# A three-layer graph network on one core: node-times-weight products as three float32r products instead of float32, with the last group's products moved in between them

## The chip, the core and the metric

The kernel runs on one core of a Trainium2 chip. The metric is the device time of one launch in microseconds (us); lower is better. The engines named below are TensorE (PE, with its weight loads shown apart as PEld), VectorE (DVE), ScalarE (ACT), GpSimd (POOL) and SyncE (SP), which here only issues DMAs. Each engine works through its own list of instructions in order.

## What is computed

2500 nodes with 256 features each, 80000 edges `src -> dst`, three layers with weights of 512 x 256, and a last weight of 1024 x 256:

```python
h = max(layernorm(x), 0)
xs = [h]
for W, b in ((W0, b0), (W1, b1), (W2, b2)):
    m = concatenate([h[dst], h[src] - h[dst]]) @ W + b     # per edge
    h = relu(segment_sum(m, dst) / max(count(dst), 1))     # per node
    xs.append(h)
out = x + concatenate(xs) @ Wf + bf
```

The kernel counts the edges into a matrix A (nodes by nodes, count of edges) and works on whole nodes: a layer is A times (nodes times the lower half of W), scaled, plus nodes times the difference of both halves; the last weight is applied layer by layer.

## The kernel before

The nodes are padded to 20 tiles of 128 (`NT`), and kept transposed in `hT` (feature rows, node columns) in float32. The columns of A are cut into five groups of at most 504 (`GS`); four of them form two pairs, and the fifth, with 486 columns, is `alone`. A float32 product appears in the trace as two matmul instructions; a float32r one, whose operands keep fewer bits, as one.

The time falls into stages, each bound to the next by the values of `hT`:

- Up to about 62 us: edges, layer norm, the first node products, and the first counts.
- To 204.97 us: layer 0. Counts are made with bf16 one-hot products, and multiplied with the node products at once. The node products are kept as two float32r parts, `zh` and `zl`, whose sum is the float32 value.
- Layers 1 and 2, each in three parts, in the loop that starts at line 1194:
  - **nodes**: `nodes_pair` (line 1000) for ten pairs of tiles `t, t + Q`. PE multiplies `hT` with the lower half of W (`ws[l][1]`, tile name `wb`) into one PSUM bank, ACT scales it with `share` into `zf`, ACT and DVE split it into `zh` and `zl`, DVE forms four sums of its quarters (`combine`, line 989), which are split into `sh` and `sl`. `final` (line 758) multiplies the same tiles of `hT` with that layer's part of the last weight (`wfs[l]`, tile name `wf`) and DVE adds the product to `acc`, the output being gathered.
  - **lone group**: `Alone` (line 1115), first in the `Stream` (line 1158): 80 float32r matmuls of the split nodes with the fifth group, then the group's own product with `ws[l][0]` (tile name `wt`) and its relu on ACT.
  - **pairs**: `Pair` (line 1028), 2 x 5 x 7 steps: a seven-product scheme of the kind of Strassen and Winograd. A step has four float32r matmuls of 504 columns. Its moving operand, a `block`, is made by ACT (a cast of what SP loaded into `staged`) or by DVE (a sum of two such blocks), up to six steps ahead; `ready` has seven buffers for it. At the last of each five, `take` (line 1089) adds the products up into `hT`.
- `final(L, t)` for all 20 tiles, with the output's DMAs.

`tick` (line 1207) adds the bias `bf_sb` to `acc` on DVE in four instructions, in layer 1 at steps 6 to 9, which are steps of the lone group. All calls through `DVEo`, `ACTo`, `POOLo`, `PEo` and `SPo` keep the order of the program on their engine, and the names `tmp`, `staged`, `block` and `bank` are pools of buffers: an instruction that writes one waits until its last reader is done.

Of the kernel before, what the change touches and what calls it, by code (L numbers as in the profile page):

```python
# [313 lines left out]
def by_windows(ctx: ExitStack, tc: tile.TileContext, x, src, dst, Ws, bs, Wf, bf, out, missing):  # L314
# [122 lines left out]
    wfs = [None] * (L + 1)  # L437

    def load_wb(l, queue=SP):
        ws[l] = wpool.tile([P, DC, D], F32, name="wt"), wpool.tile([P, DC, D], F32, name="wb", bufs=1)  # L440
        queue.dma_start(ws[l][1], Ws[l][D:2 * D, :].rearrange("(c p) d -> p c d", p=P))
# [4 lines left out]
    def load_wf(l, queue=SP):  # L446
        wfs[l] = wpool.tile([P, DC, D], F32, name="wf", bufs=1)
        queue.dma_start(wfs[l], Wf[l * D:(l + 1) * D, :].rearrange("(c p) d -> p c d", p=P))
# [309 lines left out]
    def final(l, *ts):  # L758
        po = bank()
        for i, t in enumerate(ts):  # L760
            for c in range(DC):
                PEo.matmul(po[:, i * D:(i + 1) * D], hT[:, c, t * P:(t + 1) * P], wfs[l][:, c, :],
                           start=(c == 0), stop=(c == DC - 1))
        for i, t in enumerate(ts):
            DVEo.scalar_tensor_tensor(acc[:, t, :], po[:, i * D:(i + 1) * D], share[:, t:t + 1], acc[:, t, :],
                                      op0=OP.mult, op1=OP.add)
            if l == L:
                n = P if t < NT - 1 else LAST
                SPo.dma_start(out[t * P:t * P + n, :], acc[:n, t, :])

# [148 lines left out]
    ps_left = ctx.enter_context(tc.tile_pool(name="ps_left", bufs=4, space=PSUM))  # L919
    head[0].close()  # L920
    ps_right = ctx.enter_context(tc.tile_pool(name="ps_right", bufs=4, space=PSUM))
# [46 lines left out]
    def bank():  # L968
        ps.append(ps_left if ps[-1] is ps_right else ps_right)
        return ps[-1].tile([P, 512], F32, name="bank")  # L970

    tmps = ctx.enter_context(tc.tile_pool(name="tmps", bufs=6))
    stage = ctx.enter_context(tc.tile_pool(name="stage", bufs=3))
# [7 lines left out]
    S3, S5, S2, S4 = range(4)  # L981
    SEVEN = (("x", 0, 0), "b11"), (("x", 0, 1), "b21"), (("s", S4), "b22"), (("s", S5), "r1"), \
        (("s", S2), "r2"), (("s", S3), "r3"), (("x", 1, 1), "r4")
# [5 lines left out]
    def combine(to, x):  # L989
        DVEo.tensor_sub(to[:, S3:S5 + 1, :], x[:, 0::3, :], x[:, 1:2, :].to_broadcast([P, 2, P]))  # L990
        DVEo.scalar_tensor_tensor(to[:, S2, :], to[:, S5, :], -1.0, x[:, 0, :], op0=OP.mult, op1=OP.subtract)
        DVEo.scalar_tensor_tensor(to[:, S4, :], x[:, 2, :], -1.0, to[:, S2, :], op0=OP.mult, op1=OP.subtract)

    def both_of(z, t):
        return z[:, t % 2, :Q * D].rearrange("p (i q d) -> p i q d", i=2, d=D)[:, :, t // 2, :]

    def sums_of(z, t):
        return z[:, t % 2, t // 2 * 2 * D:(t // 2 + 1) * 2 * D]

    def nodes_pair(l, t):  # L1000
        two = t, t + Q
        pz = bank()
        for i, u in enumerate(two):
            for c in range(DC):
                PEo.matmul(pz[:, i * D:(i + 1) * D], hT[:, c, u * P:(u + 1) * P], ws[l][1][:, c, :],
                           start=(c == 0), stop=(c == DC - 1))
        zf = tmp()
        for i, u in enumerate(two):
            part = slice(i * D, (i + 1) * D)
            if u == NT - 1:  # L1010
                DVEo.scalar_tensor_tensor(zf[:, part], pz[:, part], share[:, u:u + 1], brow[:, l % 2, :],
                                          op0=OP.mult, op1=OP.add)
            else:
                ACTo.activation(zf[:, part], pz[:, part], AF.Copy, scale=share[:, u:u + 1])
        ACTo.copy(both_of(zh, t), zf.rearrange("p (h d) -> p h d", h=2))
        raw = tmp()
        combine(raw.rearrange("p (s n) -> p s n", s=4), zf.rearrange("p (s n) -> p s n", s=4))
        ACTo.copy(sums_of(sh, t), raw)
        DVEo.tensor_sub(both_of(zl, t), zf.rearrange("p (h d) -> p h d", h=2), both_of(zh, t).bitcast(F32))
        final(l, *two)  # L1020
        DVEo.tensor_sub(sums_of(sl, t), raw, sums_of(sh, t).bitcast(F32))

    def part_of(what, z, j):
        if what[0] == "x":
            return tile_of((zh, zl)[z], j + what[2] * Q)[:, what[1] * P:(what[1] + 1) * P]
        return sums_of((sh, sl)[z], j)[:, what[1] * P:(what[1] + 1) * P]

    class Pair:
# [6 lines left out]
        def load(self, c):  # L1035
            st = stage.tile([P, 4, 2, GS], BF16, name="staged")
            j = 2 * c
            for i, g in enumerate(pairs[self.i]):
                SPo.dma_start(st[:, 2 * i:2 * i + 2, :, :],
                              a_dram[g].rearrange("p (h j) n -> p h j n", h=2)[:, :, j:j + 2, :])  # L1040
            return st

        def make(self, c, what, st, made):
            to = made[what] = ready.tile([P, 2, GS], F32R, name="block")
            b11, b21, b12, b22 = (st[:, i, :, :] for i in range(4))
# [4 lines left out]
            elif what == "r2":  # L1050
                DVEo.tensor_add(to, made["r1"].bitcast(F32), b22)
            elif what == "r3":
                DVEo.tensor_sub(to, made["r2"].bitcast(F32), b11)
            else:
                DVEo.tensor_add(to, made["r2"].bitcast(F32), b21)

        def own_sum(self, i):
# [7 lines left out]
            elif i == 2:  # L1065
                r["r3"] = tmp()[:, :GS]
                DVEo.tensor_sub(r["r3"], r["r2"], hT[:, 0, one])
# [21 lines left out]
        def take(self, what):  # L1089
# [6 lines left out]
            elif what == "b22":  # L1096
                self.f = tmp()[:, :GS]
                DVEo.tensor_add(self.f, m, self.e1)
# [16 lines left out]
    class Alone:  # L1115

        def __init__(self, l):
            self.l = l
            self.c0, self.n = group_of(alone)

        def load(self, c):
            st = stage.tile([P, 4, 2, GS], BF16, name="staged").rearrange("p a b n -> p (a b) n")[:, :4, :]
            SPo.dma_start(st, a_dram[alone][:, 4 * c:4 * c + 4, :])
            return st

        def make(self, c, i, st, made):
            made[i] = ready.tile([P, 2, GS], F32R, name="block")
            ACTo.copy(made[i], st[:, 2 * i:2 * i + 2, :])

        def multiply(self, c, i, made):  # L1130
            n = self.n
            if c == 0 and i == 0:
                self.banks = [bank(), bank()]
            for k in range(2):
                t = 4 * c + 2 * i + k
                for o in range(DC):
                    for z in (zh, zl):
                        unit[0] = PEo.matmul(self.banks[o][:, :n], tile_of(z, t)[:, o * P:(o + 1) * P],
                                             made[i][:, k, :n], start=(t == 0 and z is zh), stop=False)
            if c == 4 and i == 1:  # L1140
                for o in range(DC):
                    for cc in range(DC):
                        PEo.matmul(self.banks[o][:, :n], ws[self.l][0][:, cc, o * P:(o + 1) * P],
                                   hT[:, cc, self.c0:self.c0 + n], start=False, stop=(cc == DC - 1))
                for o in range(DC):
                    ACTo.activation(hT[:, o, self.c0:self.c0 + n], self.banks[o][:, :n], AF.Relu)

    def steps_of(l):
        steps, loads = [], []
        for p in Alone(l), Pair(l, 0), Pair(l, 1):  # L1150
            for c in range(5) if isinstance(p, Pair) else (0, 1, 3, 2, 4):
                loads.append((p, c))
                made = {}
                for part, what in SEVEN if isinstance(p, Pair) else ((None, 0), (None, 1)):
# [3 lines left out]
    class Stream:  # L1158
# [19 lines left out]
        def run(self, tick, between):  # L1178
            for n, (m, p, c, part, what, made) in enumerate(self.steps):
                for then in between.get(n, ()):  # L1180
                    then()
                self.make(n + LEAD + 1)
                if isinstance(p, Pair):
                    if c == 2:
                        p.own_sum([w for _, w in SEVEN].index(what) - 2)
                    p.multiply(c, part, what, made)
                    if c == Q // 2 - 1:
                        p.take(what)
                else:
                    p.multiply(c, what, made)  # L1190
                tick(n)

    DVEo.tensor_sub(ws[1][0], ws[1][0], ws[1][1])
    for l in range(1, L):
        stream = Stream(l)
        stream.load(3)
        for i, t in enumerate(range(Q) if l == 1 else [6, 0, 1, 2, 3, 4, 5, 7, 8, 9]):
            nodes_pair(l, t)
            if i == 6:
                stream.make(2)  # L1200
        load_wf(l + 1, SPo)
        if l + 1 < L:
            load_b(l + 1, SPo)
            load_wb(l + 1, SPo)
            load_wt(l + 1, SPo)

        def tick(n):
            if l == 1 and 6 <= n < 10:
                part = acc[:, (n - 6) * 5:(n - 5) * 5, :]
                DVEo.tensor_add(part, part, bf_sb.unsqueeze(1).to_broadcast([P, 5, D]))  # L1210

        def sums_of_w():
# [46 lines left out]
```

## Time and profile before

Three runs: 493.4, 493.45 and 494.22 us, the median 493.45. The profiled execution took 493.74 us; its span, from the first to the last instruction, is 491.9.

| Stage (from the trace) | from us | to us | PE busy | PEld busy | DVE busy | ACT busy | POOL busy |
|---|---|---|---|---|---|---|---|
| nodes, layer 1 | 204.97 | 239.30 | 34.33 | 30.22 | 27.27 | 21.44 | 0 |
| lone group, layer 1 | 239.30 | 259.90 | 20.60 | 16.57 | 13.60 | 11.82 | 0 |
| nodes, layer 2 | 336.40 | 370.70 | 34.30 | 30.19 | 28.57 | 22.80 | 0 |
| last products | 467.60 | 485.60 | 17.45 | 15.01 | 10.36 | 1.98 | 0 |

A row is a stretch of the span, and its entries are the time in it in which each engine had an instruction at work. PE is busy through every one of these stretches; the other engines have time to spare in each. PE's durations overlap[...], so a matmul's cost is read from the distance of two starts ("pitch"), not from its duration. Over the whole span the granted TensorE clock was 0.997 of full speed.

### The profile page before, as it was taken

The numbers are of one execution on the slowest core, as the hardware profiler recorded it, in microseconds if no ns is written. First come the engines' busy times: TensorE is split into PE (matmuls) and PEld (weight loads), VectorE is DVE, ScalarE is ACT, GpSimd is POOL, SyncE is SP. The second block draws the span as 40 slices with busy tenths as digits, with TensorE's granted clock in tenths as the row PEclk, the third lists the DMA queues.
The fourth block names the chain that finished last, engine by engine and source line by source line (L and its number), as shares of the span: only waits on it lengthen the run. The fifth ranks groups of instructions, "written<-read, shape, count | busy, mean of one in ns | idle before, by whom it ended". The sixth has DMA issues, their size and how long they took to land.

```text
span 491.9 us, 7411 instructions
## 1 busy us (share of the span) xinstructions
PE 481.7 (98%) x2776; PEld 384.0 (78%) x2776; DVE 366.6 (75%) x767; ACT 241.3 (49%) x445; POOL 43.2 (9%) x66
## 2 busy tenths in 40 slices
PE   8999999999999999999999999999999999999994
PEld 4888888778778778788887867868888788688683
DVE  8999988888888861087955959867883469689552
ACT  5676677653734340257745445425578344364010
POOL 3682006100101000000000000000000000000000
PEclk9999999999999999999999999999999999999998
DMA  9310098970914609300472552420015534340033
GB/s 289 106 43 1 2 203 153 204 150 0 184 29 86 127 5 205 130 1 7 141 253 85 168 168 76 136 85 1 1 42 162 202 121 142 111 144 26 0 116 100
DMA packets 26679, 51.73 MB, mean 105 GB/s; under 512 B 1945, under 2 KB 22378, under 8 KB 26602
## 3 DMA queue, kind: packets, MB, share of 16 engines
q1 hardware_dynamic: 19850, 33.54, 20.8%
q0 software_dynamic: 5856, 16.51, 17.6%
q10 hardware_dynamic: 928, 1.11, 0.7%
q8 instruction: 24, 0.39, 0.3%
q14 instruction: 21, 0.17, 0.1%
HBM read 35.69 MB, written 16.10 MB: 105 GB/s over the span
## 4 chain that ended last, share of the span: by engine, by line
PE 91%; DVE 3%; POOL 3%; DMA 1%; issue 1%; SPq 0%; POOLq 0%
PE bank L282 87%; PE pz L282 3%; POOL acc L282 2%; DMA acc<-in_x_dram 1%; DVE st L282 1%; POOL ed L282 1%; POOL es L282 0%; DVE mv L282 0%; PE turned L282 0%; DVE zl L282 0%; DVE rs L282 0%; DVE off L282 0%; DVE away L282 0%; DVE one_m L282 0%; DVE kn L282 0%
## 5 line engine op out<-in xcount | busy, mean ns | idle before, releaser
L282 ACT CAST block<-staged 128x1008 fp32r<-128x1008 bf16 x80 | 77.6, 1031 | 40.9 <-issue 38.2
L282 PE MATMUL bank<-a,zh 128*128 128x504 f32 (+1 forms) x200 | 84.3, 422 | 0.0
L282 PE MATMUL bank<-block,zh 128*128 128x504 f32 (+1 forms) x200 | 83.4, 417 | 0.0
L282 DVE TENSOR_TENSOR one_m<-iota_m,key_m 128x1024 bf16<-128x1024 bf16 (+1 forms) x105 | 72.0, 686 | 14.1 <-PE bank L282 14.0
L282 ACT CAST a<-bank 128x480 fp32r<-128x480 f32 (+1 forms) x105 | 52.9, 565 | 59.3 <-PE bank L282 59.3
L282 PE MATMUL bank<-a,zl 128*128 128x504 f32 (+1 forms) x200 | 77.8, 389 | 0.0
L282 PE MATMUL bank<-block,zl 128*128 128x504 f32 (+1 forms) x200 | 77.6, 388 | 0.0
L282 DVE TENSOR_TENSOR block<-block,staged 128x1008 fp32r<-128x1008 f32 x60 | 70.8, 1205 | 4.9 <-PE bank L282 1.7
L282 PE MATMUL bank<-block,sh 128*128 128x504 f32 x160 | 68.7, 429 | 0.0
L282 DVE TENSOR_TENSOR one_n<-iota_n,key_n 128x480 bf16<-128x480 bf16 (+1 forms) x210 | 66.9, 359 | 0.0
L282 PE MATMUL bank<-block,sl 128*128 128x504 f32 x160 | 62.5, 391 | 0.0
L282 PE MATMUL bank<-wf,hT 128*128 128x256 f32 x240 | 55.2, 379 | 0.0
L282 PEld LDWEIGHTS bank<-wf,hT 128*128 128x128 f32 x240 | 45.6, 190 | 6.2
L282 DVE TENSOR_TENSOR block<-staged 128x1008 fp32r<-128x1008 bf16 x20 | 24.1, 1205 | 32.1 <-PE bank L282 32.1
L282 PEld LDWEIGHTS <-one_m 128*128 128x128 bf16 x834 | 39.1, 98 | 9.6 <-issue 3.2
L282 PEld LDWEIGHTS bank<-a,zh 128*128 128x128 f32 x200 | 37.8, 189 | 10.7 <-issue 2.6
L282 PEld LDWEIGHTS bank<-block,zh 128*128 128x128 f32 x200 | 37.7, 188 | 10.2 <-issue 3.2
L282 PEld LDWEIGHTS bank<-block,zl 128*128 128x128 f32 x200 | 37.6, 188 | 10.2 <-issue 3.2
L282 PEld LDWEIGHTS bank<-a,zl 128*128 128x128 f32 x200 | 37.7, 189 | 9.0 <-issue 2.6
L282 PE MATMUL bank<-one_n,one_m 128*128 128x120 bf16 x834 | 44.2, 208 | 0.0
L282 PE MATMUL bank<-wb,hT 128*128 128x256 f32 x160 | 37.8, 379 | 0.0
L282 PEld LDWEIGHTS bank<-block,sl 128*128 128x128 f32 x160 | 30.1, 188 | 9.7 <-issue 3.7
(144 smaller groups left out, 574.6 us busy)
## 6 DMA issues: line engine op xcount, KB each, us to landing
staged<-a_dram SPq DMA_DIRECT2D x50, 504.0 KB
a_dram<-a POOLq DMA_DIRECT2D x20, 630.0 KB, 7.5
out_dram<-acc SPq DMA_DIRECT2D x19, 128.0 KB
acc<-in_x_dram POOLq DMA_DIRECT2D x3, 640.0 KB, 11.8
wf<-in_L_gnn_Wf_dram SPq DMA_DIRECT2D x4, 256.0 KB
acc<-in_x_dram SPq DMA_DIRECT2D x1, 896.0 KB
acc<-in_x_dram ACTq DMA_DIRECT2D x1, 768.0 KB
wb<-in_L_gnn_W_dram SPq DMA_DIRECT2D x3, 256.0 KB
```

The source lines that it names most:

```text
L282: return self.tc.keep_in_program_order(call(*args, **kwargs))
```

## The change

The diff has four parts.

1. **Products.** A row of `hT` is cut into a high part and a rest, both short enough for float32r (`Split`: three parts, high, low, and a combination of both), and so are the weights (`Forms`: three parts). Three float32r matmuls then give what a float32 matmul gave (`times`). The weight `wb` and the last weight's part `wf` lie side by side in one tile (`raws`), so one matmul has 512 columns: the left 256 become the nodes' product, the right 256 the output's. In layer 1 the first two pairs of tiles are still multiplied in float32 (`times_whole`). The last stage has `wf` alone, 256 columns.
2. **Order of nodes and lone group.** A pair is now the tiles `2q, 2q+1`. In step i of twelve, PE multiplies the i-th pair of tiles and then the lone group's blocks with the nodes of step i-2; the lone group is no longer part of the `Stream`.
3. **Engines.** `combine` in the nodes (now three instructions) and the subtraction in `Split.low` are on POOL; the bias is added on POOL in layer 1 at steps 2, 6, 10 and 14 of the pairs. Some splits and the forms of the next stage are made during the last steps of the pairs.
4. **Buffers.** The PSUM banks are handed out anew for nodes (six, and two for the lone group) and pairs (eight); `stage` has four buffers instead of three, and `Split` takes its parts from it; a pair's load takes four neighbouring tiles of a group instead of two and two.

The signs of the seven-product scheme change with the order of the quarters; its steps and sizes do not.

```diff
     def load_wb(l, queue=SP):
-        ws[l] = wpool.tile([P, DC, D], F32, name="wt"), wpool.tile([P, DC, D], F32, name="wb", bufs=1)
+        raws[l] = wpool.tile([P, DC, 2, D], F32, name="wbf", bufs=1)
+        ws[l] = wpool.tile([P, DC, D], F32, name="wt"), raws[l][:, :, 0, :]
...
-    def combine(to, x):
-        DVEo.tensor_sub(to[:, S3:S5 + 1, :], x[:, 0::3, :], x[:, 1:2, :].to_broadcast([P, 2, P]))
-        DVEo.scalar_tensor_tensor(to[:, S2, :], to[:, S5, :], -1.0, x[:, 0, :], op0=OP.mult, op1=OP.subtract)
-        DVEo.scalar_tensor_tensor(to[:, S4, :], x[:, 2, :], -1.0, to[:, S2, :], op0=OP.mult, op1=OP.subtract)
+    def combine(to, x, V):
+        V.tensor_sub(to[:, M3:S5 + 1, :], x[:, 1::2, :], x[:, 0:2, :])
+        V.tensor_sub(to[:, S2, :], to[:, M3, :], x[:, 3, :])
+        V.tensor_add(to[:, M4, :], to[:, S2, :], x[:, 2, :])
...
+    class Split:
...
+        def high(self):
+            ACTo.activation(self.parts[0], self.h, AF.Copy, scale=DOWN)
+        def low(self, V):
+            V.tensor_sub(self.parts[1], self.h, self.parts[0].bitcast(F32))
+        def across(self, V):
+            V.scalar_tensor_tensor(self.parts[2], self.parts[1].bitcast(F32), -E12, self.parts[0].bitcast(F32),
+                                   op0=OP.mult, op1=OP.add)
+    class Forms:
...
+        def high(self):
+            ACTo.activation(self.parts[0], self.raw, AF.Copy, scale=C1 * DOWN)
+        def low(self):
+            for c in range(DC):
+                self.V.scalar_tensor_tensor(self.rest[c], self.raw[:, c, :], C1, self.parts[0][:, c, :].bitcast(F32),
+                                            op0=OP.mult, op1=OP.subtract)
...
+    def times(to, split, i, forms):
+        for c in range(DC):
+            for k in range(3):
+                PEo.matmul(to, split.parts[k][:, c, i * P:(i + 1) * P], forms.parts[k][:, c, :],
+                           start=(c == 0 and k == 0), stop=(c == DC - 1 and k == 2))
...
+    def split(q, V=POOLo):
+        sp = splits[q] = Split(q)
+        sp.high()
+        sp.low(V)
+        sp.across(DVEo)
...
     for l in range(1, L):
+        order = orders[l]
+        whole = 2 if l == 1 else 0
+        lone = Alone(l, order, banks(6, 2))
+        if l == 1:
+            load_alone(0, order)
+            split(order[whole])
+            forms = Forms(flat(l), 512, DVEo, [tmp(), tmp()])
+            forms.high()
+            forms.low()
+            forms.scaled()
+            forms.across()
+            forms.last()
...
+        for i in range(Q + LAG):
+            if 0 < i <= Q:
+                lone.make(i - 1)
+            if i < Q:
+                q = order[i]
+                n = Nodes(l, q)
+                n.multiply(None if i < whole else splits.pop(q), forms, flat(l))
+                if i + AHEAD_H < Q and i % 2 == 1:
+                    load_alone((i + 1) // 2, order)
+                n.parts()
+                n.combine(POOLo)
+                if i + AHEAD_H < Q and order[i + AHEAD_H] not in splits:
+                    split(order[i + AHEAD_H])
+                pending.append(n)
+            if i and pending:
+                pending.pop(0).sums()
+            if i >= LAG:
+                lone.multiply(i - LAG)
+            if i == Q - 1:
+                load_alone(Q // 2 - 1, order)
+                stream.load(3)
+        stream.make(2)
+        lone.end()
...
         def tick(n):
-            if l == 1 and 6 <= n < 10:
-                part = acc[:, (n - 6) * 5:(n - 5) * 5, :]
-                DVEo.tensor_add(part, part, bf_sb.unsqueeze(1).to_broadcast([P, 5, D]))
+            if l == 1 and 2 <= n < 18 and n % 4 == 2:
+                part = acc[:, (n - 2) // 4 * 5:(n + 2) // 4 * 5, :]
+                POOLo.tensor_add(part, part, bf_sb.unsqueeze(1).to_broadcast([P, 5, D]))
...
+            if n in (49, 56):
+                split(after[(n - 49) // 7])
+            if n == 63:
+                if l + 1 < L:
+                    load_alone(0, after)
+                else:
+                    split(after[3])
+            if n == 65:
+                split(after[2])
...
-    for t in [*range(7), NT - 4, NT - 3, NT - 2, NT - 1, *range(7, NT - 4)]:
-        final(L, t)
+    order = orders[L]
+    for i, q in enumerate(order):
+        po, sp = bank(), splits.pop(q)
+        for k in range(2):
+            times(po[:, k * D:(k + 1) * D], sp, k, forms)
+        for k in range(2):
+            t = 2 * q + k
+            add_to_acc(t, po[:, k * D:(k + 1) * D])
+            n = P if t < NT - 1 else LAST
+            SPo.dma_start(out[t * P:t * P + n, :], acc[:n, t, :])
+        for k in order[i + 1:i + 4]:
+            if k not in splits:
+                split(k)
```

`Nodes.parts` has the ACT and DVE work of `nodes_pair` without the sums (two scalings and the cast to `zh` on ACT, the subtraction to `zl` and two additions to `acc` on DVE), `Nodes.sums` the cast to `sh` and the subtraction to `sl`. The methods of `Forms` come in the order `high` (ACT), `low` (DVE, two instructions of 512 columns), `scaled` (ACT, two), `across` (DVE, two), `last` (ACT, two). The forms of the next stage are made by them in `tick` at steps 64, 66 and 67.

## The prediction

> **What bounds the kernel now.** I read first the page's shares and slices, then the chain of waits, then the stretches and the order of time where the change works.
>
> ```profile
> PE 481.7 (98%) x2776; PEld 384.0 (78%) x2776; DVE 366.6 (75%) x767; ACT 241.3 (49%) x445; POOL 43.2 (9%) x66
> ...
> PE   8999999999999999999999999999999999999994
> ...
> PEclk9999999999999999999999999999999999999998
> ...
> PE 91%; DVE 3%; POOL 3%; DMA 1%; issue 1%; SPq 0%; POOLq 0%
> ```
>
> PE is busy in every slice, at full clock, and the chain of the end is PE for 91%: from 62 us to 485 it is one piece. So a matmul saved in these stages is time saved, until another engine is late. The order of time gives what a matmul costs:
>
> ```profile
> 336.38 1.89 PE L282 MATMUL bank<-wb,hT 128*128 128x256 f32 x8
> 338.10 1.89 PE L282 MATMUL bank<-wf,hT 128*128 128x256 f32 x8
> ```
>
> ```profile
> 371.13 0.39 PE L282 MATMUL bank<-block,zl 128*128 128x486 f32 x1
> 371.35 0.38 PE L282 MATMUL bank<-block,zh 128*128 128x486 f32 x1
> ...
> 467.62 17.43 PE L282 MATMUL bank<-wf,hT 128*128 128x256 f32 x80
> ```
>
> Eight float32 instructions of 256 columns start every 1.726 us: 0.216 each, two to a product. A float32r matmul (the zl and zh rows) of 486 columns has a pitch of 0.220; in the pairs, 504 columns, 0.229. Per column that is 0.454 ns against 2 x 0.216 / 256 = 1.69 for a float32 product: three float32r products are 1.36, a fifth less.
>
> **The PE sum.** A tile now takes 8 instructions for `wb` and `wf`: 1.726 us. New: two feature halves x 3 x 512 columns x 0.454 = 6 x 0.232 = 1.39. Saved 0.334 a tile; 16 tiles in layer 1 (four stay float32, at 512 columns as dear as before) and 20 in layer 2: **12.0 us**. In the last stage a tile falls from 4 x 0.216 = 0.863 to six matmuls of 256 columns. No row has that width in float32r. Below, 256 x 0.454 = 0.116; above, the duration of its weight load, 0.190, if it can't overlap. The transposes have loads of the same 128 columns at a pitch of 0.108, so the stream should decide; as the excess over 2.4 columns per ns was 18 ns at both 486 and 504 columns, I take 256 / 2.4 + 18 = 0.125. Saved 0.863 - 0.75 = 0.113, x 20 = **2.3 us**. The stall of 0.19 before each lone group (pitch 0.41 for 0.22) goes too: 0.4. PE sum: **-14.7 us**. The lone group's 80 matmuls and its own product are only moved.
>
> **What replaces it.** In a step of the new nodes PE needs 12 x 0.232 + 8 x 0.220 = 4.54 us. Against that, by pitch from the rows of the old nodes:
> - ACT: two scalings 0.87, casts to zh and sh 0.5 each, Split.high like a cast 0.5, one lone block 0.94: 3.3. Hidden.
> - DVE: zl and sl 0.6 each, two additions to acc 0.79, Split.across about 0.66 (the 512-column two-input rows): 2.65. Hidden, but in order: across waits for POOL's low, and sl and the next zl stand behind it.
> - POOL: 256 + 128 + 128 columns of combine, 512 of low. POOL has run no two-input instruction in this trace. The nearest row is its normalisation, one tensor in:
>
> ```profile
> L282 POOL TENSOR_SCALAR acc<-acc,rs,off x16: 550/707/1469, 15.3 to 39.4; 128x256 f32<-128x256 f32 x16
> ```
>
> ```profile
> 22.86 2.18 POOL L282 TENSOR_SCALAR acc<-acc,rs,off 128x256 f32<-128x256 f32 x2
> ```
>
> ```profile
> 22.11 0.68 DVE L282 TENSOR_TENSOR one_m<-iota_m,key_m 128x1024 bf16<-128x1024 bf16 x1
> 22.71 0.64 DVE L282 TENSOR_TENSOR one_n<-iota_n,key_n 128x480 bf16<-128x480 bf16 x2
> 23.26 0.97 DVE L282 TENSOR_TENSOR one_m<-iota_m,key_m 128x1024 bf16<-128x1024 bf16 x1
> ```
>
> Undisturbed it takes 0.55 for 256 columns (2.15 ns each), beside DVE's two-input compares up to 1.47, and the compare takes 0.97 instead of 0.68 as POOL runs: they get in each other's way. Two inputs cost between the row's 2.15 and twice that, 4.3 ns. The Trainium skill (GPSIMD Engine Reference, 3.1 Elementwise) says 2.6 cycles per element for a two-input instruction, an estimate of 2.17 ns; I take this, the low end, as it names the very instruction, with 0.1 each on top: 1024 x 2.17 + 0.4 = **2.6 us**, plus at most two waits of 0.53 for DVE: 3.7 of 4.54. Hidden. The same page's 4.1 (Engine selection) speaks against the change: elementwise work of two inputs belongs on VectorE, POOL being about twice as slow. By it moving combine costs more than it frees; the old nodes' rows say DVE would have 2.65 + 1.0 (combine) + 0.6 (low) = 4.25 of 4.54, hardly any room, so POOL is the better place as long as its 3.7 holds.
>
> Where PE waits all the same:
> - **Start of layer 1: +2.3.** The forms' buffers come free only as layer 0 ends. ACT does relu, Split.high, forms; DVE waits for POOL's first low (1.2), then low, across: about 7 us, just what the two float32 pairs take (4 x 1.726 = 6.9). But behind the forms on ACT's queue stand the evacuations of pairs 0 and 1 and the next Split.high, 3.9 us; then POOL, low of pair 3 behind combine of pair 1, 2.2; across 0.8: 13.9 us after layer 0. PE is there at 6.9 + 2.78 + 1.76 = 11.4. Layer 2 has three splits made before: +0.4. No bound below zero; above, with POOL at 4.3 ns, 6 and 3.5.
> - **Bias on POOL: +3.1.** Four instructions of 1280 columns, 2.9 us each. They wait for no step of the pairs, so they run when POOL is free after the last combine, some 5 us before the pairs begin, just when DVE makes the first four sums of blocks (1.2 each, two SBUF inputs). The row: a POOL instruction of 0.55 cost the compare 0.29, half its time. With two inputs read I take three quarters: 2.1 us each, 8.6 in all, if one gets in ahead of each sum. DVE has 10.6 us for 5.2 of work: 8.6 - 5.4 = 3.2 late. The Trainium skill (SBUF — State Buffer, Who interferes with whom) has an exclusive lock for the whole instruction: 4 x 2.9 - 5.4 = 6. If the half holds: 5.8 - 5.4, 0.4. I take 3.1, and the ends 0 and 6. The old place, DVE in the lone group, cost nothing, as DVE was idle there.
> - **End of the pairs: +0.7 each layer.** At steps 49 and 56 DVE waits for POOL's low (1.2 + across 0.66), twice; the blocks are five steps ahead, 4.5 us, DVE has 1.5 us to spare in seven steps of 6.4 and the own sums need 2.7. Forms (2.6 us on DVE) come when no block is left to make.
> - **Last stage: +0.6.** DVE has 0.79 for every pair and 0.66 for six splits, ACT and POOL one instruction, PE 1.5. Only the fifth split, behind two relus on ACT, is late.
>
> The loads on SP's queue change in order, not in bytes; the first load of the pairs is asked for some 8 us before its use, beside a stage buffer that a split frees. The output's DMAs follow 15 us of additions instead of 17; the tail of 6.3 us behind the last addition stays.
>
> **Sum**: -14.7 + 2.3 + 0.4 + 3.1 + 1.4 + 0.6 = -6.9. The profiled execution of before took 493.74 (span 491.9), so 486.8; it lay 0.3 above the median, so I say **486.6 us**.
>
> **Rivals.**
> 1. *Everything hidden*: POOL nearer 1.5 ns, the lock cheap, the bias free. -14.7 + 2.3 = -12.4: **481 us**. For it: the undisturbed POOL row, and DVE's slack in all stages.
> 2. *POOL becomes the bound* in nodes: 1024 x 3 ns + 0.4 + waits of 1.06 = 4.54, so it decides from 3 ns on, and there the gain is about gone. At 4 ns a step takes 5.6, +1.1 in 14 steps = 15; starts 9.5, bias 5: 29.5 - 14.7 = +15, **508 us**. For it: twice the one-input row. Against: the page's figure, and the 0.55 row includes its own start.
> 3. *Weight loads bound float32r at 256 columns*: 120 x (0.190 - 0.125) = +7.8: **494.5 us**. Against: the transposes' pitch of 0.108.
> 4. *The change doesn't do what it says*, the 512-column float32r running slower than its 504-column row: 12.0 gone at 0.288; no row speaks for it.
>
> **Chances.** Forecast 0.40, its own range 482 to 492; all hidden 0.22; POOL bound 0.24; weight loads 0.10; others 0.04. This kernel's runs tell about 0.2% (1 us) from no change. Faster: 0.40 + 0.22 + 0.02 = 0.64; within 0.2%: 0.05, mostly of case 3; slower 0.31. Range **480.5 to 506**: up to case 2 nearly, down past case 1.
>
> **What would show it.** Float32r rows of 512 columns at a pitch of 0.232 and of 256 at 0.125; nodes and lone group together about 52 us in layer 1 and 49 in layer 2, where now it is 55; gaps of PE at the fourth pair of layer 1 and at the pairs' steps 5 and 6, released by DVE. POOL two-input rows: 512 columns at 1.2 us, or 2 where case 2 holds, and then PE waiting for DVE behind POOL in every step. The forecast is wrong if these rows stand above 1.6 us or the gaps lie elsewhere.

## The result, and the profile after

Four runs of the changed kernel: 495.88, 496.18, 496.89 and 497.67 us, median 496.53. Beside them the kernel before had a median of 493.69. The ratio is 1.0059, with a 95% interval of 1.0037 to 1.0081: slower by 0.6%, where a gain of 1.4% was forecast.

From the page of the changed kernel: busy time by engine, the slices of PE and of its granted clock, the chain that ended last.

```profile
span 494.0 us, 7493 instructions
...
PE 474.3 (96%) x2728; PEld 367.5 (74%) x2728; DVE 391.7 (79%) x743; ACT 264.6 (54%) x488; POOL 142.9 (29%) x158
...
PE   8999999999999999989996999999999999999994
...
PEclk9999999999999999999997999999999999999998
...
PE 64%; issue 13%; DVE 11%; POOL 6%; ACT 3%; DMA 2%; SPq 0%; DVEq 0%; POOLq 0%; ACTq 0%
```

PE has 7.4 us less to do than before (481.7), yet the span is 2.1 us longer. One slice of PE now stands at 6, and one slice of the clock at 7; PE's part of the chain fell from 91% to 64%. So the products did become cheaper, and PE now waits. Where, the stretches show: first the kernel before, then the changed one, each from the first node product of a layer. The columns are start:end, length, busy time (and count) of PE, PEld, DVE, ACT and POOL, granted clock, DMA share, GB/s.

```profile
204.97:260.00 55.03, 55.03 (x248) 46.80 (x247) 40.96 (x81) 33.36 (x54) 0.00 (x0) 1.00 0.32 109
260.00:336.40 76.40, 76.40 (x311) 58.13 (x310) 57.36 (x61) 31.53 (x36) 0.00 (x0) 1.00 0.36 116
336.40:391.50 55.10, 55.10 (x250) 46.84 (x248) 37.32 (x80) 34.68 (x55) 0.00 (x0) 1.00 0.24 81
391.50:467.60 76.10, 76.10 (x310) 58.07 (x309) 56.97 (x59) 31.43 (x36) 0.00 (x0) 1.00 0.29 95
```

```profile
206.00:258.10 52.10, 50.76 (x200) 37.48 (x200) 37.74 (x54) 39.37 (x65) 38.94 (x40) 1.00 0.36 119
258.10:343.60 85.50, 79.50 (x309) 59.11 (x309) 76.45 (x75) 37.93 (x45) 13.63 (x6) 0.96 0.27 91
343.60:393.10 49.50, 49.07 (x208) 38.95 (x208) 34.43 (x52) 36.66 (x60) 32.25 (x37) 1.00 0.40 134
393.10:471.00 77.90, 76.71 (x309) 57.85 (x309) 63.50 (x70) 36.18 (x44) 5.52 (x4) 1.00 0.25 85
```

Rows 1 and 3 of each fence are nodes and lone group, rows 2 and 4 are the pairs. Nodes and lone group take 2.9 and 5.6 us less; up to the start of the group's own product, a mark that both kernels share, it is 3.4 and 6.0. The pairs of layer 1, which the diff hardly touches, take 9 us more: DVE is busy there for 76.45 us instead of 57.36, and the clock falls to 0.96. Two things make nearly all of that loss, and the second of them costs at other places too.

**The bias on POOL.** The order of time of the changed kernel at the pairs' first steps, on DVE, then on PE (start, duration, engine, line, operation, tiles and shape, count; in brackets the idle time before and what ended it):

```profile
256.36 3.89 DVE L282 TENSOR_TENSOR block<-staged 128x1008 fp32r<-128x1008 bf16 x1
260.35 3.78 DVE L282 TENSOR_TENSOR block<-block,staged 128x1008 fp32r<-128x1008 f32 x1
264.24 3.72 DVE L282 TENSOR_TENSOR block<-staged,block 128x1008 fp32r<-128x1008 bf16 x1
267.88 1.19 DVE L282 TENSOR_TENSOR block<-block,staged 128x1008 fp32r<-128x1008 f32 x1
```

```profile
264.19 0.50 PE L282 MATMUL bank<-block,sh 128*128 128x504 f32 x1 [1.33 <-DVE block L282]
...
268.01 0.79 PE L282 MATMUL bank<-block,sh 128*128 128x504 f32 x1 [2.63 <-DVE block L282]
268.60 0.62 PE L282 MATMUL bank<-block,sl 128*128 128x504 f32 x1
269.02 0.62 PE L282 MATMUL bank<-block,sh 128*128 128x504 f32 x1
```

While POOL adds the bias (four instructions, 252.48 to 266.89), a sum of blocks lasts 3.7 to 3.9 us; once POOL is done, 1.19. PE comes to blocks that aren't made: two waits, which lengthen the distance of two starts from 0.23 to 1.72 and to 3.02. Then something that no step of the forecast had: after the second wait PE's matmuls start 0.42 apart instead of 0.229. The stretches show the granted clock behind it:

```profile
262.00:265.00 3.00, 1.67 (x8) 1.05 (x6) 2.90 (x2) 1.09 (x2) 3.00 (x2) 1.00 0.00 0
265.00:268.00 3.00, 0.39 (x2) 0.00 (x0) 3.00 (x2) 0.00 (x0) 1.89 (x1) 0.64 0.00 0
268.00:270.00 2.00, 1.99 (x5) 1.63 (x6) 1.93 (x5) 0.00 (x0) 0.00 (x0) 0.50 0.00 0
```

The clock is at half speed when PE resumes, and full again only at 272.7. Between the starts at 262.47 and 272.74 lie 16 distances, which at 0.229 would make 3.66 us; they make 10.27. The loss is 6.6 us, 4.4 in the two waits and 2.2 in the slow matmuls after.

**The PSUM banks.** Each time the banks are handed out anew, PE stops. The end of layer 0 in the changed kernel, PE and then ACT:

```profile
201.91 3.42 PE L282 MATMUL bank<-hT,wt 128*128 128x486 f32 x8
206.00 1.55 PE L282 MATMUL bank<-wbf,hT 128*128 128x512 f32 x3 [0.67 <-ACT hT L282]
```

```profile
205.37 0.58 ACT L282 ACTIVATE hT<-bank 128x486 f32<-128x486 f32 x1 [0.24 <-PE bank L282]
```

The first node product waits until ACT has read the last bank of the old stage (205.95), though it writes a bank that was free long before. The last product starts at 204.76 and the next at 206.00: 1.24 us, where 0.41 is usual. It is the same at all four places where banks are handed out: 0.83, 0.83, 1.03 and 0.83 us lost, **3.5** in all.

### The profile page after: what moved, and what is told of

Read it like the earlier page. It is cut to its first block, busy times and chain, and to the rows that moved or that the text cites. A ratio compares the mean times of both kernels' runs of the same rounds, so it can differ in the third digit from the quotient of the medians.

```text
span 494.0 us, 7493 instructions
## 1 busy us (share of the span) xinstructions
PE 474.3 (96%) x2728; PEld 367.5 (74%) x2728; DVE 391.7 (79%) x743; ACT 264.6 (54%) x488; POOL 142.9 (29%) x158
## 4 chain that ended last, share of the span: by engine, by line
PE 64%; issue 13%; DVE 11%; POOL 6%; ACT 3%; DMA 2%; SPq 0%; DVEq 0%; POOLq 0%; ACTq 0%
PE bank L282 60%; DVE block L282 5%; PE pz L282 3%; POOL staged L282 2%; POOL acc L282 2%; DMA acc<-in_x_dram 1%; DVE staged L282 1%; DVE tmp L282 1%; POOL tmp L282 1%; DMA staged<-a_dram 1%; DVE st L282 1%; ACT hT L282 1%; POOL ed L282 1%; POOL es L282 0%; ACT block L282 0%
## 5 line engine op out<-in xcount | busy, mean ns | idle before, releaser
L282 ACT CAST block<-staged 128x1008 fp32r<-128x1008 bf16 x80 | 79.3, 1031 | 44.2 <-issue 42.8
L282 POOL TENSOR_TENSOR staged<-hT,staged 128x512 fp32r<-128x512 f32 x28 | 39.9, 1434 | 167.8 <-ACT staged L282 167.8
L282 PE MATMUL bank<-block,sh 128*128 128x504 f32 x160 | 69.9, 437 | 4.0 <-DVE block L282 4.0
L282 PE MATMUL bank<-block,staged 128*128 128x512 f32 (+1 forms) x336 | 69.8, 358 | 3.5 <-DVE staged L282 2.1
L282 PEld LDWEIGHTS bank<-block,staged 128*128 128x128 f32 x336 | 55.1, 188 | 15.5 <-DVE staged L282 3.9
L282 POOL TENSOR_TENSOR tmp<-tmp 128x128 f32<-128x128 f32 (+1 forms) x60 | 46.0, 766 | 31.2 <-ACT tmp L282 24.7
L282 DVE SCALAR_TENSOR_TENSOR staged<-staged 128x512 fp32r<-128x512 f32 x28 | 22.6, 807 | 39.5 <-POOL staged L282 39.5
L282 DVE TENSOR_TENSOR block<-block,staged 128x1008 fp32r<-128x1008 f32 x40 | 52.5, 1313 | 1.4
L282 POOL DMA_DIRECT2D a_dram<-a x20 | 10.7, 542 | 127.7 <-ACT a L282 127.4
```

What stands on the lines that cost most here:

```text
L282: return self.tc.keep_in_program_order(call(*args, **kwargs))
```

## The experiments

Times are medians, ratios are to the kernel before on the same chip, with a 95% interval. Sums of waits are PE's distances of starts beyond the usual pitch, in the profiled execution.

**1. The bias left out** (`a1_no_bias`).

```diff
-            if l == 1 and 2 <= n < 18 and n % 4 == 2:
-                part = acc[:, (n - 2) // 4 * 5:(n + 2) // 4 * 5, :]
-                POOLo.tensor_add(part, part, bf_sb.unsqueeze(1).to_broadcast([P, 5, D]))
```

> The changed kernel without the four bias additions on POOL; the bias is left out of the output (it is zero in these inputs). Theory[...]: the first four sums of blocks in layer 1's pairs fall from 3.8 us to 1.2, the gaps of PE at steps 4 to 6 (1.5 + 2.8 us) and the slow TensorE clock after them (about 2 us) go, 6.9 us less in all: some 489 us. Rival (the gaps are late loads or the new start of the pairs, and POOL only happens to run then): 494 to 496 us, gaps where they were.

489.85 us, ratio 0.994 (0.9918 to 0.9961): 1.2% below the changed kernel's ratio. The profiled span is 5.9 us shorter, and layer 0 happened to end 0.7 later in it: 6.6, as read above. The waits and the slow clock at the pairs' start are both gone. The same sum of blocks in this kernel:

```profile
257.13 1.21 DVE L282 TENSOR_TENSOR block<-staged,block 128x1008 fp32r<-128x1008 bf16 x1
```

Nothing but the POOL instructions was taken away, so they are what made these sums 3.7 to 3.9 us long, and what slowed PE.

**2. The bias on DVE** (`a3_bias_dve`): the other way to free the pairs' start, with nothing left out. DVE adds the bias at four steps of the pairs where it is ahead.

```diff
-            if l == 1 and 2 <= n < 18 and n % 4 == 2:
-                part = acc[:, (n - 2) // 4 * 5:(n + 2) // 4 * 5, :]
-                POOLo.tensor_add(part, part, bf_sb.unsqueeze(1).to_broadcast([P, 5, D]))
+            if l == 1 and n in (9, 23, 25, 44):
+                k = (9, 23, 25, 44).index(n)
+                part = acc[:, k * 5:(k + 1) * 5, :]
+                DVEo.tensor_add(part, part, bf_sb.unsqueeze(1).to_broadcast([P, 5, D]))
```

> The bias on VectorE at steps 9, 23, 25 and 44 of layer 1's pairs, 1.4 us each. Theory: VectorE has 1.5 us to spare in every seven steps and the blocks are up to six steps ahead, so this costs nothing on PE: as without the bias, some 489 us. Rival (VectorE is full there, the work itself is too much): 1.5 to 5 us of new gaps at these steps, 491 to 494 us.

490.17 us, 0.9954 (0.994 to 0.9968): as without any bias, within the intervals. So it isn't the addition that costs, but its engine and place.

**3. The bias on POOL in pieces** (`b4_bias_pieces`): does the length of one POOL instruction matter, or POOL's work as such? Twenty instructions of 256 columns instead of four of 1280.

```diff
-            if l == 1 and 2 <= n < 18 and n % 4 == 2:
...
+            if l == 1 and n < NT:
+                POOLo.tensor_add(acc[:, n, :], acc[:, n, :], bf_sb)
```

> The changed kernel with the bias on POOL in 20 pieces of 256 columns instead of four of 1280. Theory (what hurts is that one instruction keeps VectorE out for 2.7 us while the blocks' lead is small): each sum of blocks is kept up by some 0.55 us at most, the gaps at steps 4 to 6 fall below 1.5 us in all and the TensorE clock stays high, 491 to 492 us. Rival (the lost VectorE time counts in sum, 20 x 0.55 = 11 us as before): 495 to 496 us.

491.99 us, 0.9989 (0.9975 to 1.0003). From the order of time, POOL and one of DVE's sums:

```profile
255.25 25.77 POOL L282 TENSOR_TENSOR acc<-acc,bf_sb 128x256 f32<-128x256 f32 x18
```

```profile
275.27 1.74 DVE L282 TENSOR_TENSOR block<-block,staged 128x1008 fp32r<-128x1008 f32 x1
```

A sum now takes 1.54 to 1.75 instead of 1.2: it waits for one short instruction and not for a long one. POOL's additions stretch over more than 25 us, since each waits in turn for a sum. The large waits and the slow clock are gone (clock 0.998), smaller waits come later, at 281 to 286 us, 1.8 together. DVE doesn't lose much less in all: the same thirty instructions, from the last two of the nodes' on, last 8.9 us longer than in experiment 1, where the four long additions make it 10.3. But the loss comes as some 0.3 to 0.55 at a time over 28 us, and so falls in part where DVE has time to spare (in experiment 1 it idles 3.15 us before its sum at 263.59), instead of all at once at the pairs' start, where the blocks' lead over PE is small. The place on DVE is better still.

**4. Banks kept** (`a2_kept_banks`): the banks come from two standing pools in turn, as before the change; all else as changed.

```diff
-    def banks(n, alone=0):
-        nonlocal banks_of
-        banks_of.close()
...
+    def bank():
+        ps.append(ps_left if ps[-1] is ps_right else ps_right)
+        return ps[-1].tile([P, 512], F32, name="bank")
...
-            self.to = [pool.tile([P, 512], F32, name="bank")[:, :self.n] for _ in range(DC)]
+            self.to = [bank()[:, :self.n] for _ in range(DC)]
...
-        banks(8)
```

> The changed kernel with the PSUM banks handed out from the two pools of layer 0 all along, none closed and opened again. Theory (opening a pool makes the first matmul wait for the last reader of every bank of the old one): the four gaps of 0.83, 0.83, 1.03 and 0.83 us at 204.8, 257.7, 342.4 and 392.7 us fall to nothing, 3.5 us less: some 493 us. Rival (PE waits there for values that it needs, hT or the first block): the gaps stay, 496 us.

497.14 us, 1.0089 (1.0066 to 1.0112): no faster, a miss. The four stops are gone from the trace, 3.5 us, and 1.9 of it, in layer 2, is kept. In layer 1 PE merely arrives sooner at the waits that follow: the one at the fourth pair grows from 0.76 to 1.68, the first one of the bias from 1.49 to 2.39. And after the longer wait at the fourth pair stands a slow clock that was not there before. Two stretches of this kernel (the waits, then what follows), and PE in them:

```profile
216.59:220.00 3.41, 1.14 (x5) 0.39 (x3) 2.08 (x4) 3.38 (x7) 3.25 (x5) 1.00 0.37 87
220.00:223.42 3.42, 3.42 (x9) 2.65 (x10) 3.03 (x6) 1.57 (x3) 2.63 (x3) 0.50 0.16 64
```

```profile
218.63 0.50 PE L282 MATMUL bank<-block,staged 128*128 128x512 f32 x1 [1.51 <-POOL staged L282]
219.89 4.15 PE L282 MATMUL bank<-block,staged 128*128 128x512 f32 x10 [0.76 <-DVE staged L282]
```

Ten matmuls last from the second wait for 4.15 us; the changed kernel ran the same ten in 2.59.

**5. Both** (`a4_banks_and_bias`): the edits of 2 and 4 together.

> Both together: banks kept and the bias on VectorE. Theory: the two costs lie at different places and add, 3.5 + 6.9 us less than the change: some 486 us, 7 to 8 us below the kernel before. Rival (one hides behind the other): 488 us or more.

487.1 us, 0.9889 (0.987 to 0.9908). Against experiment 2 the kept banks now bring 3.1 us of the 3.5 that the four stops cost, although the first wait at the fourth pair again grows by 0.9. So the stops were worth most of that, but not while the bias and the slow clock behind them took it back. The two waits at the fourth pair stand here just as in experiment 4, and the clock stays up:

```profile
219.04 0.50 PE L282 MATMUL bank<-block,staged 128*128 128x512 f32 x1 [1.52 <-POOL staged L282]
220.31 2.59 PE L282 MATMUL bank<-block,staged 128*128 128x512 f32 x10 [0.77 <-DVE staged L282]
```

Three stretches of the same length as those in experiment 4, in this kernel:

```profile
215.45:218.86 3.41, 2.07 (x10) 1.42 (x8) 1.48 (x3) 3.38 (x7) 3.10 (x5) 1.00 0.02 5
218.86:222.27 3.41, 2.46 (x10) 1.80 (x10) 3.25 (x4) 3.10 (x6) 3.25 (x5) 1.00 0.52 151
222.27:225.69 3.42, 3.42 (x17) 2.83 (x16) 3.01 (x5) 2.72 (x5) 2.92 (x4) 1.00 0.00 0
```

In experiment 4 both waits fall into one such stretch, and PE is busy for 1.14 us of it; here they fall into two, with 2.07 and 2.46. Why these stretches are the ones that count is worked out in the last section.

**6. Float32 again** (`b3_float32`): experiment 5 with the products in float32 in the new order: no `Split`, no `Forms`.

```diff
-        whole = 2 if l == 1 else 0
+        whole = Q
...
-            times(po[:, k * D:(k + 1) * D], sp, k, forms)
+            times_whole(po[:, k * D:(k + 1) * D], 2 * q + k, flat(L))
```

> On top of a4_banks_and_bias, the products in float32 again (all pairs as the first two of layer 1, the last stage at 256 columns), in the new order, without Split and Forms. Theory: PE +12.0 in the nodes and about +0.9 in the last stage, less the gaps that the splits made (3.2 + 0.8 + 1.8 + 1.1): 487.1 + 12.9 - 6.9 = some 493 us, so the three products bring 6 us net, and order and banks alone nothing. Rival (most of a4's gain comes from the new order, not from the products): 489 us or less.

492.96 us, 0.9992 (0.9983 to 1.0). Order, banks and bias alone bring nothing that can be told; against experiment 5 the three products are worth 5.9 us, splits, forms and their waits paid.

**7 and 8. Which of POOL's parts belong there** (`b1_low_dve`, `b2_all_dve`): experiment 5 with `Split.low` on DVE, and then with `combine` on DVE as well.

```diff
-    def split(q, V=POOLo):
+    def split(q, V=DVEo):
```

> On top of a4_banks_and_bias, Split.low on VectorE instead of POOL, everywhere. Theory (the gaps at the fourth pair of layer 1, the fourth of layer 2, the pairs' steps 60 to 62 and the last stage are VectorE waiting for POOL's low, 1.4 us where VectorE takes 0.6): the gaps of 3.2, 0.8, 0.9 each and 1.1 us shrink to about half or less, 4 us less: some 483 us. Rival (VectorE has no room for 28 more instructions): new gaps in the steps of nodes, 487 us or more.

484.83 us, 0.9845 (0.9824 to 0.9865): 2.3 better than experiment 5. The waits at the start of layer 1 fall from 2.8 to 1.0, those at the start of layer 2 vanish; four waits of 0.58 appear in the last stage, where DVE also adds to `acc`.

```diff
-                n.combine(POOLo)
+                n.combine(DVEo)
```

> On top of b1_low_dve, combine on VectorE too, so that POOL has no part in layers 1 and 2. The skill's rule (elementwise work of two inputs belongs on VectorE): zl, sl and across lose their waits for POOL and VectorE fits in a step (4.25 of 4.54 us), so as fast as b1_low_dve or faster, 482 to 484 us. Rival (my sum: hardly any room, and in order): PE waits in the steps of nodes, 0.3 to 1 us in each of 16, 487 to 498 us.

487.94 us, 0.9892 (0.9873 to 0.9912), 3.1 worse than with `combine` on POOL (2.6 between the profiled executions). PE at the fourth pair of layer 1, with `combine` on POOL and then on DVE:

```profile
217.19 0.50 PE L282 MATMUL bank<-block,staged 128*128 128x512 f32 x1 [0.23 <-DVE staged L282]
```

```profile
218.55 0.50 PE L282 MATMUL bank<-block,staged 128*128 128x512 f32 x1 [1.23 <-DVE staged L282]
```

In the steady steps DVE manages all of it without a wait of PE. At the starts, where every split is awaited, `combine` stands before it in DVE's queue: 1.0 us more in layer 1 and 1.1 in layer 2. The rest is not placed. So the rule that the expectation tested held for `low` and not for `combine`; its rival has the time right, but the waits lie at the starts and not in the steps.

**9. A mixture** (`c1_mixed`): experiment 7, but with `low` on POOL in the last stage, and the bias on DVE at steps 2, 9, 23 and 25 of the pairs.

```diff
-                split(k)
+                split(k, POOLo)
```

> b1_low_dve with two moves: Split.low on POOL in the last stage only (where VectorE has the additions to acc and shows four gaps of 0.6 us, POOL one of 1.1), and the bias on VectorE at steps 2, 9, 23 and 25 instead of 9, 23, 25 and 44 (the gap near step 62 of layer 1 is 1.1 us, without a bias before it, in layer 2, 0.5). Theory: 0.6 + 0.6 us less, some 483.6 us. Rival (the gap near step 62 is the splits' alone, and POOL is late in the last stage): 484.8 us or more.

484.18 us, 0.9809 (0.9791 to 0.9827): 1.9% faster than the kernel before, and faster than the changed one. From its page:

```profile
span 481.1 us, 7470 instructions
...
PE 470.9 (98%) x2728; PEld 366.5 (76%) x2728; DVE 390.7 (81%) x769; ACT 263.8 (55%) x488; POOL 95.5 (20%) x132
```

PE's share is back at the 98% it had before the change. In its last stage PE never stands idle for more than 0.02 us. Against experiment 7 (0.9824 to 0.9865) the intervals overlap, so the mixture itself is not shown to be better.

## Why the prediction was wrong

**Right: the products.** A float32r matmul of 512 columns has a mean pitch of 0.232 us, as worked out; one of 256 columns 0.120 in the median and 0.129 in the mean, against 0.125. (The 2.4 columns per ns behind that 0.125 can be read in the trace of before: bf16 matmuls of 512 columns on the tile `idle` start 0.215 us apart.) So weight loads don't bound it (rival 3), and a float32r of 512 columns is no slower than its neighbour of 504 (rival 4). Experiment 9 bears the sum out: in its trace, layer 1's nodes and lone group, from the first node product to the start of the group's own product, take 47.8 us against 52.2 before, layer 2's 45.6 against 52.2, the last stage 15.6 against 17.3. That is 12.7 us, with 1.0 still lost to waits at the start of layer 1: 13.7 of the 14.7.

One saving of that sum was never there: the 0.4 for "the stall of 0.19 before each lone group". In the trace of before the last float32 matmul starts at 370.70, the first float32r one 0.03 us later and the next 0.41 after that. The 0.44 together are just the two usual pitches, 0.216 and 0.220; only the start between them is recorded early. Without the stall the PE sum is 14.3, and the forecast from its own rows 6.5 instead of 6.9.

**Right: POOL's price, so rival 2 falls.** The view of the tile `staged` on POOL in the changed kernel (shortest, median, longest in ns):

```profile
L282 POOL TENSOR_TENSOR staged<-hT,staged x28: 1269/1297/1746, 206.7 to 482.5; 128x512 fp32r<-128x512 f32 x28
```

I said 1.2. With the shortest of the 128-column ones, 0.458, the shortest of 512 gives 2.11 ns for an element and 0.19 for the instruction, against 2.17 and 0.1 assumed. Over a whole step POOL is no bound. But rival 1, all hidden, is not what happened either: at the starts each split is on the path, and moving `low` to DVE (experiment 7) brought 2.3 us. The price was right and the place not the best.

**Right: the starts and the ends of the pairs.** Start of layer 1: 2.3 forecast; measured 0.76, 1.02 and 0.11 at the fourth pair, where the gaps were foretold: 1.9. Start of layer 2: 0.4 forecast, 0.7 measured. The end of the pairs: 0.7 forecast, 0.9 measured in each layer. The forecast of 52 and 49 us for nodes and lone group stands beside 52.1 and 49.5. Last stage: 15.6 forecast, 16.5 measured: one wait of 1.06 at the fifth split, the one that was named, was given 0.6, and the mean pitch of 0.129 instead of 0.125 makes the other 0.5.

**Wrong: "Bias on POOL: +3.1".** The mechanism was right and its place too, steps 5 and 6; the size was 6.6. (By its own working, 8.6 - 5.4, the term is 3.2.) Two parts of it failed. First the lock: "With two inputs read I take three quarters: 2.1 us each". What DVE lost is 2.5 to 2.7 us on each instruction (3.72 to 3.89 less 1.2), out of some 2.9 that a POOL instruction of 1280 columns takes by the prices above (an estimate; in the trace, with its own waits for DVE, it lasts 3.6). This is nearly the whole of it, as the Trainium skill says (SBUF — State Buffer, Who interferes with whom), and not what the one-input normalisation had led me to. With 10.3 us lost on four DVE instructions (`sl`, then three sums) instead of 8.6, and the same slack of 5.4, DVE is 4.9 late; PE waited 4.4. Second, 2.2 us of slow clock behind the waits, for which the sum had nothing. The end of 6 that I gave for the page's rule was near the truth, partly for another reason.

**Wrong: no term for the banks.** The sum lists where PE waits all the same, and the re-opened pools are not on the list, though the change was described with them. They cost 3.5 us. The trace of before could not show it, but the list of parts could have asked it: each of the four openings makes the next product wait for the last reader of the stage before, one bank's evacuation (0.58 on ACT, and the product before it).

From the forecast's -6.9 to the +2.1 of the profiled execution it is 9.0. Of these, 3.5 are the banks, 3.5 the bias, 0.4 the ends of the pairs, 0.9 the last stage and 0.4 the stall that wasn't there, while the starts of the layers were 0.1 cheaper than said: 8.6. The last 0.4 are not placed (layer 0's end alone varied by 0.7 between two profiles).

## What to carry to other kernels

Cost every part of a diff, the handing out of buffers too: pools opened anew at a stage's boundary tie the first write of the new stage to the last read of the old one, at each boundary. When work is moved to POOL, count the whole length of its longest instruction against any two-input instruction of DVE beside it, and put it where DVE has that much slack, or cut it into pieces, which spreads DVE's loss rather than lessening it. And where several small waits follow one another, taking one away may only lengthen the next: judge such an edit with the next wait removed as well, as experiments 4 and 5 show.

## What the runs showed of the hardware

PE's clock went down after waits shorter than I had counted with. After a wait of 1.33 us, four matmuls, and another of 2.63 it was at 0.50; full speed came back after about 4.7 us of matmuls, which cost 2.2. The Trainium skill (TensorE: Matmul & The Clock Gate, Part 1) puts it at one idle window of some 3.4 us that runs freely. Here no wait was that long, and nor is the length of the wait all: 1.51 and 0.76 us with one matmul between them brought the clock to 0.50 in experiment 4, while 1.52 and 0.77 at the same place left it at 1.00 in experiment 5.

The eleven kept traces agree with the page on the window and show how empty it has to be. In each, from the first full speed on, every stretch at one speed, the last one apart, lasts a whole number of times 3.41 us: in the changed kernel 76 times, then 2 at half speed, then 64. I cut each trace by this step and counted PE's busy time in every piece. After each of the 14 pieces with PE busy for 48% or less, the next one ran at half speed; after each of the other 1528, busy for 57% or more, at full speed. The changed kernel's two, and the emptiest one that kept the clock, in experiment 8 (`b2_all_dve`) at the fourth pair:

```profile
262.42:265.83 3.41, 1.64 (x6) 0.68 (x5) 3.31 (x2) 0.67 (x1) 3.41 (x2) 1.00 0.00 0
265.83:269.25 3.42, 1.24 (x3) 1.06 (x4) 3.42 (x3) 0.00 (x0) 1.06 (x1) 0.50 0.00 0
269.25:272.66 3.41, 3.41 (x9) 2.68 (x9) 3.13 (x6) 0.00 (x0) 0.00 (x0) 0.50 0.73 229
```

```profile
216.03:219.45 3.42, 1.97 (x8) 1.12 (x7) 3.32 (x9) 3.39 (x7) 0.00 (x0) 1.00 0.32 73
219.45:222.86 3.41, 3.41 (x16) 2.79 (x17) 3.31 (x9) 2.51 (x5) 0.00 (x0) 1.00 0.19 78
```

So in these traces several waits add up if they fall into one window, and the same waits cost nothing in clock if a boundary parts them, as in experiments 4 and 5. Where the first full speed begins differs from trace to trace (4.4 to 7.4 us after the start), so a single profile may show either case by luck. The mean clock was 0.983 to 0.987 in the four runs of experiment 4, 0.990 to 0.993 in those of the changed kernel and 0.993 to 0.999 in experiment 5, so all four of the first had more slow time; where, only the profiled one shows. No run moved the window on purpose, and the ends of matmuls, on which the busy times rest, are modelled.
